# A state-space layer with four states side by side on the partitions, and a symmetric incidence matrix of which half is transposed instead of computed

## The chip, the core and the metric

The kernel runs on one core of a Trainium2 chip. The core has five engines with a queue of instructions each, and every queue is worked off in its order: PE (matrix products; its loads of the stationary operand are listed as PEld), DVE (vector work), ACT (activation functions and copies), POOL (a second, slower vector engine, which reads and writes SBUF only), and SP, which here only starts transfers (DMA). PE writes to PSUM, eight banks of 128 x 512 fp32; a tile of 128 x 512 fp32 fills one bank.

The metric is the time of one execution on the device in microseconds (us). Three runs of the kernel before took 5677.81, 5738.25 and 5755.19 us, with a median of 5738.25 us.

## The reference, cut to what matters

The program is a stack of four layers on a batch of 4 images with 128 channels and 64 x 64 pixels (4096 positions). Layers 2 and 3 (attention and mixtures of experts) are not touched by the change; only layers 0 and 1 are.

```python
# layer 0: a selective state-space scan, 256 inner channels d, 16 states n, along 4096 positions t
dA = exp(dt_t[:, :, None] * A)                         # A: 256 x 16
hn = dA * hprev + (dt_t * x_t)[:, :, None] * B_t[:, None, :]
y  = einsum('bdn,bn->bd', hn, C_t)                     # sum over the 16 states
...
y = (y + xc * D) * silu(zg);  out = y @ out_proj_w.T + x
# layer 1, on the group-normalised x: a hypergraph of 4096 tokens
d2 = sq[:, :, None] + sq[:, None, :] - 2.0 * einsum('bic,bjc->bij', xf, xf)
incidence = (sqrt(maximum(d2, 0)) < 16.0)              # 4096 x 4096 zeros and ones
edge = einsum('bve,bvc->bec', incidence, xe) / deg_e   # xe = xf @ W_fc.T + b_fc
vert = einsum('bve,bec->bvc', incidence, edge) / deg_v
out  = vert + xf;  then a batch norm over all images and silu
```

Two properties carry the change. In layer 0 each of the 256 x 16 scans is independent of the others, and B and C depend on the state and the position but not on the channel. In layer 1 the distances, and so the incidence matrix, are symmetric.

## The kernel before, in words

All matrix operands are fp32 but for the incidence matrix (zeros and ones in fp8) and the fp16 pairs (a high and a low part) that it is multiplied with.

**Layer 0** works on chunks of 512 positions: 8 chunks for each of 4 images. For a chunk, `before` issues four steps (load x; project through the convolution, L189 to L193; a small product that gives dt, B and C, L200 to L203; delta, L212 to L219). `state(s, n)` then handles one state for all 256 channels, which lie as two halves on the 128 partitions. A transfer on SP's queue (L235) spreads rows B and C of that state over all 128 partitions (tile `bt`, four buffers). POOL multiplies dt*x by B (`db`, L237, 128 x 1024). For each half ACT computes exp(dt*A) into a PSUM bank (`dA`, L241), and DVE runs the recurrence as a scan over 512 positions (`hs`, L243). ACT keeps the last column for the next chunk (`carry`, L245), DVE multiplies by C (`hc`, L247, 128 x 1024, all operands in SBUF), and PE sums over the states by two products with the identity matrix that accumulate in PSUM over the 16 states (`y`, L249). So a chunk has 16 states, 32 scans and 32 such products. `after` adds the skip term, multiplies by the gate on POOL (L258), projects out (L262), and stores the layer's output to device memory from ACT's queue.

**Layer 1** of an image builds the incidence matrix in 8 panels of 512 columns. A panel has 32 blocks of 128 x 512: `compare` computes a product on PE (`ps_g`, L358) and DVE compares it with the norms and writes zeros and ones (`inc`, L361). All 32 x 8 blocks are computed. `edges` multiplies the finished panel with the tokens (`ps_ed`, L370: 4 x 32 products of 258 columns a panel), in a PSUM bank of its own. Six of the eight panels are stored to device memory (L412) and loaded again (L423) for the second pass, which multiplies the panels with the edge features (`ps_v`, L436: 64 products of 512 columns a panel) in the same extra bank. The eight normalised chunks `xn` stay in SBUF from their load to the end of the image.

**The order of the work.** Layer 0 of image 0 is issued alone. Then layer 0 of image b+1 and layer 1 of image b are issued interleaved: after each of the 128 state steps as much of layer 1 is issued as its weighted work asks for. Layer 1 of image 3 stands alone at the end. The compiler's scheduler then fixes the order on each engine; tiles with the same tag share their buffers, and an instruction that needs a buffer waits for its last user. PSUM is divided into 3 banks `ps` for all passing products, 1 bank for `edges` and the second pass, 2 for `dA` and 2 for `y`.

Of the kernel before, what the change touches and what calls it, by code (L numbers as in the profile page):

```python
# [7 lines left out]
F32 = mybir.dt.float32  # L8
# [30 lines left out]
class Net:  # L39
# [33 lines left out]
    def layers01(self):  # L73
# [5 lines left out]
        with ExitStack() as ctx:  # L79
            wp = ctx.enter_context(tc.tile_pool(name="aw", bufs=1))  # L80
            w2 = ctx.enter_context(tc.tile_pool(name="l0p", bufs=2))
            bcp = ctx.enter_context(tc.tile_pool(name="l0bc", bufs=4))
            tp = ctx.enter_context(tc.tile_pool(name="l1t", bufs=2))
            dp = ctx.enter_context(tc.tile_pool(name="l0d", bufs=3, space=DRAM))
            ip = ctx.enter_context(tc.tile_pool(name="l1i", bufs=1, space=DRAM))

            ps = ctx.enter_context(tc.tile_pool(name="aps", bufs=3, space=PSUM))
            eps = ctx.enter_context(tc.tile_pool(name="l1e", bufs=1, space=PSUM))
            aps = ctx.enter_context(tc.tile_pool(name="l0a", bufs=2, space=PSUM))
            yps = ctx.enter_context(tc.tile_pool(name="l0y", bufs=1, space=PSUM))  # L90
# [8 lines left out]
            A = wp.tile([P, 2, DS], F32, tag="A", name="A")  # L99
            carry = wp.tile([P, DS, 2], F32, tag="carry", name="carry")  # L100
# [4 lines left out]
            top = wp.tile([P, 1], F32, tag="top", name="top")  # L105
            with tc.tile_pool(name="l0t", bufs=2) as tp0:
# [15 lines left out]
                nc.scalar.dma_start(A, a["L0_conv_A_log"].rearrange("(k p) n -> p k n", p=P))  # L122
                nc.scalar.activation(A, A, AF.Exp)
                nc.vector.tensor_scalar(A, A, -1.0, None, ALU.mult)
                for h in range(2):
# [13 lines left out]
                    self.transposed(ps, xpT[:, h, :], xw[:, h * P : (h + 1) * P])  # L139
# [28 lines left out]

            def before(b, c):
# [12 lines left out]
                def project():  # L182
                    xt = s["xt"]
                    xc = s["xc"] = w2.tile([P, 2, T], F32, tag="xc", name="xc")
                    zs = s["zs"] = w2.tile([P, 2, T], F32, tag="zs", name="zs")
                    for h in range(2):
# [4 lines left out]
                        pz = ps.tile([P, T], F32, tag="ps", name="ps_z")  # L191
                        nc.tensor.matmul(pz, wz[:, h, :], xt[:, 3:], start=True, stop=True)
                        nc.scalar.activation(zs[:, h, :], pz, AF.Silu)  # L193

                def small():
                    xc = s["xc"]
                    xd = s["xd"] = w2.tile([40, T], F32, tag="xd", name="xd")
# [5 lines left out]
                    nc.scalar.dma_start(bcd, xd[DR:40, :])  # L203

                def delta():

                    xd = s["xd"]
                    dl = s["dl"] = w2.tile([P, 2, T], F32, tag="dl", name="dl")
# [8 lines left out]
                    nc.gpsimd.tensor_tensor(dl, dl, sp, ALU.add)  # L217
                    dx = s["dx"] = w2.tile([P, 2, T], F32, tag="dx", name="dx")
                    nc.gpsimd.tensor_tensor(dx, dl, s["xc"], ALU.mult)  # L219

                return s, [load, project, small, delta]

            def state(s, n):


                c, dl, dx, bcd = s["c"], s["dl"], s["dx"], s["bcd"]
                if n == 0:
                    s["y"] = [yps.tile([P, T], F32, tag=f"y{h}", name=f"y{h}") for h in range(2)]
                y = s["y"]

                bt = bcp.tile([P, 2, T], F32, tag="bt", name="bt")
                rows = bass.AP(
                    tensor=bcd.tensor, offset=bcd[n : n + 1, :].offset, ap=[[0, P], [DS * T, 2], [1, T]]
                )
                nc.sync.dma_start(bt, rows)  # L235
                db = w2.tile([P, 2, T], F32, tag="db", name="db")
                nc.gpsimd.tensor_tensor(db, dx, bc(bt[:, 0, :], 2), ALU.mult)  # L237
                hs = w2.tile([P, 2, T], F32, tag="hs", name="hs")
                for h in range(2):
                    dA = aps.tile([P, T], F32, tag="dA", name="dA")  # L240
# [705 lines left out]
```

## Time and profile before

The profiled execution of the kernel before has a span of 5744.0 us from its first to its last instruction; the mean clock granted to PE in it is 0.881 of full speed.

| | us |
|---|---|
| median of three runs (5677.81 to 5755.19) | 5738.25 |
| span of the profiled execution | 5744.0 |
| PE busy (81% of the span) | 4672.7 |
| DVE busy (65%) | 3714.2 |
| POOL busy (32%) | 1836.1 |
| ACT busy (31%) | 1763.0 |
| moved by DMA, MB | 502.31 |

A row of the profile's list of groups reads: line, engine, operation, what it writes and reads, the shapes, how often; then its busy time in us, the mean length of one in ns, and the idle time of the engine just before it with the instruction that ended most of it. An fp32 product appears as two records, since PE takes two passes for it: 2048 records of L249 are 1024 products. Records of products overlap at their ends, so the distance from start to start, and not the length of a record, is what a product costs on a busy PE. The clock granted to PE varies; at full clock a pass of 512 columns starts every 0.43 us.

### The profile page before, as it was taken

Reading aid. Unit: us, or ns where it says so; the run is one execution under the profiler, and the core shown is the slowest. Engines: PE = TensorE matmul, PEld = TensorE weight load, DVE = VectorE, ACT = ScalarE, POOL = GpSimd, SP = SyncE. Lnnn points to the kernel's source line nnn. Section 1 sums busy time; section 2 is a strip of 40 time slices with the busy share of each in tenths; the row PEclk is TensorE's granted clock in tenths of the full one; section 3 lists DMA queues with packets and bytes.
Section 4 is the critical chain, followed back from the end, with each engine's and each line's share of the span. In section 5 each row is a group of like instructions: output and inputs, shape, how many; then the busy total and the mean of one; then the engine's idle time right before and its main releaser. Section 6 shows DMA issues by size and latency. Waiting matters only on the chain. (4 is left out here: it accounts for less than half of the span.)

```text
span 5744.0 us, 50270 instructions
## 1 busy us (share of the span) xinstructions
PE 4672.7 (81%) x18487; PEld 2474.2 (43%) x18487; DVE 3714.2 (65%) x5227; ACT 1763.0 (31%) x2956; POOL 1836.1 (32%) x916
## 2 busy tenths in 40 slices
PE   6676688888888888888888888899986667689779
PEld 2222244444434444443444444355544555358535
DVE  6889878877647777765777876556415455438610
ACT  4544543333224333232433333210013333312220
POOL 5555544443544444344434444410121000000000
PEclk8777899999999999998999999899997788769975
DMA  4344423332343334334333332511041000150052
GB/s 103 104 109 110 109 80 99 100 100 73 111 139 86 84 105 106 69 104 138 88 91 102 90 87 85 160 66 44 23 173 49 1 1 1 56 183 1 2 185 80
DMA packets 215081, 502.31 MB, mean 87 GB/s; under 512 B 16522, under 2 KB 19122, under 8 KB 208690
## 3 DMA queue, kind: packets, MB, share of 16 engines
q1 hardware_dynamic: 203538, 479.74, 29.2%
q10 hardware_dynamic: 11296, 19.37, 1.0%
q8 instruction: 145, 2.38, 0.2%
q14 instruction: 102, 0.84, 0.1%
HBM read 421.45 MB, written 77.59 MB: 87 GB/s over the span
## 5 line engine op out<-in xcount | busy, mean ns | idle before, releaser
L237 POOL TENSOR_TENSOR db<-dx,bt 128x1024 f32<-128x1024 f32 x512 | 1282.9, 2509 | 1342.5 <-DVE hs L243 674.8
L249 PE MATMUL y<-hc,cst 128*128 128x512 f32 x2048 | 1091.8, 659 | 195.2 <-DVE hc L247 189.1
L243 DVE TENSOR_TENSOR_SCAN hs<-dA,carry,db 128x512 f32<-128x512 f32 x896 | 1103.7, 1266 | 219.7 <-POOL db L237 177.4
L358 PE MATMUL ps_g<-xn 128*128 128x512 f32 x2048 | 973.1, 611 | 131.7 <-DVE inc L361 127.9
L241 ACT ACTIVATE dA<-dl,A 128x512 f32<-128x512 f32 x1024 | 701.7, 688 | 1186.6 <-DVE hs L243 1142.1
L247 DVE TENSOR_TENSOR hc<-hs,bt 128x1024 f32<-128x1024 f32 x512 | 877.5, 1714 | 276.4 <-PE y L249 272.9
L361 DVE SCALAR_TENSOR_TENSOR inc<-ps_g,hcl,hb 128x512 fp8e4<-128x512 f32 x1024 | 733.0, 742 | 144.5 <-PE ps_g L358 105.9
L249 PEld LDWEIGHTS y<-hc,cst 128*128 128x128 f32 x2048 | 405.0, 208 | 716.8 <-issue 372.6
L358 PEld LDWEIGHTS ps_g<-xn 128*128 128x128 f32 x2048 | 382.8, 194 | 655.9 <-issue 368.1
L370 PE MATMUL ps_ed<-xs,inc 128*128 128x258 f16 x4096 | 494.8, 277 | 67.0 <-DVE ed L375 66.9
L370 PEld LDWEIGHTS <-inc 128*128 128x128 fp8e4 x4096 | 403.7, 99 | 221.5 <-issue 162.9
L436 PE MATMUL ps_v<-inc_v,es 128*128 128x512 fp8e4 x1536 | 368.3, 395 | 0.0
L436 PEld LDWEIGHTS <-es 128*128 128x128 f16 x2048 | 206.9, 101 | 282.0 <-issue 82.1
L245 ACT COPY carry<-hs 128x2 f32<-128x2 f32 x448 | 86.3, 193 | 708.1 <-DVE hs L243 705.7
L262 PE MATMUL ps_o<-xc,opT 128*128 128x512 f32 x128 | 110.2, 1011 | 180.6 <-POOL xc L258 180.5
L189 PE MATMUL ps_c<-xt,wc 128*128 128x512 f32 x512 | 240.2, 608 | 1.1 <-DMA xt<-in_x 1.1
L217 POOL TENSOR_TENSOR dl<-dl,sp 128x1024 f32<-128x1024 f32 x32 | 81.0, 2532 | 417.5 <-ACT sp L216 417.5
L243 DVE TENSOR_TENSOR_SCAN hs<-dA,db 128x512 f32<-128x512 f32 x128 | 150.8, 1206 | 61.3 <-POOL db L237 55.6
L572 PE MATMUL ps_qkT<-cst,qkv 128*128 128x128 f32 x256 | 61.8, 421 | 150.5 <-DVE qkv L566 150.5
L382 POOL TENSOR_TENSOR ed<-ed,rdeg 128x512 f32<-128x512 f32 x32 | 48.9, 1529 | 393.2 <-DVE rdeg L380 393.2
L375 DVE TENSOR_TENSOR ed<-ps_ed,ed 128x129 f32<-128x129 f32 x128 | 36.4, 285 | 201.3 <-ACT ed L374 201.1
L189 PEld LDWEIGHTS ps_c<-xt,wc 128*128 128x128 f32 x512 | 100.4, 197 | 131.2 <-issue 123.8
(246 smaller groups left out, 5165.6 us busy)
## 6 DMA issues: line engine op xcount, KB each, us to landing
bt<-bcd SPq DMA_DIRECT2D x512, 512.0 KB
inc<-inc SPq DMA_DIRECT2D x24, 2048.0 KB
inc_v<-inc SPq DMA_DIRECT2D x24, 2048.0 KB
w<-in_L_ffn_weight SPq DMA_DIRECT2D x32, 1024.0 KB
w2f<-in_L_ffn_weight SPq DMA_DIRECT2D x32, 1024.0 KB
x<-x ACTq DMA_DIRECT2D x32, 256.0 KB
xn<-x SPq DMA_DIRECT2D x32, 256.0 KB
hg<-rb SPq DMA_DIRECT2D x32, 256.0 KB
```

The lines of the kernel that those rows point to most:

```text
L189: nc.tensor.matmul(pc, wc[:, h, j, :], xt[:, j : j + T], start=j == 0, stop=j == 3)
L237: nc.gpsimd.tensor_tensor(db, dx, bc(bt[:, 0, :], 2), ALU.mult)
L241: nc.scalar.activation(dA, dl[:, h, :], AF.Exp, scale=A[:, h, n : n + 1])
L243: nc.vector.tensor_tensor_scan(hs[:, h, :], dA, db[:, h, :], init, ALU.mult, ALU.add)
L245: nc.scalar.copy(carry[:, n, :], hs[:, :, T - 1])
L247: nc.vector.tensor_tensor(hc, hs, bc(bt[:, 1, :], 2), ALU.mult)
L249: nc.tensor.matmul(y[h], self.ident, hc[:, h, :], start=n == 0, stop=n == DS - 1)
L262: nc.tensor.matmul(po, opT[:, h, :], xc[:, h, :], start=h == 0, stop=h == 1)
L358: nc.tensor.matmul(pq, xn[v // 4][:, v % 4 * P : (v % 4 + 1) * P], xn[c], start=True, stop=True)
L361: nc.vector.scalar_tensor_tensor(inc[:, v, :], pq, hc[:, v : v + 1], hb, ALU.subtract, ALU.is_gt, saturate=False)
L370: nc.tensor.matmul(pe[:, : 2 * P + 2], inc[:, v, i * P : (i + 1) * P], xs[:, v, :], start=v == 0, stop=v == NB - 1,)
L436: nc.tensor.matmul(pv, es[:, e, k, :], inc[:, e, :], start=e == 0 and k == 0, stop=e == NB - 1 and k == 1,)
```

## The change

In layer 0, a step no longer covers one state of 256 channels. It covers four states of 64 channels: the partitions hold four states of 32 channels each, and two such groups of 32 channels lie side by side in a tile (`step(s, h, q, k)`: half h, four states q, pair k of groups). There are still 16 steps a chunk, with two scans of 512 positions and one product 128 x 1024 with B and with C each. For this layout dt and dt*x, which are needed on four partition groups, are stored to device memory (`dd`, 16 small transfers a chunk) and loaded spread (`r`, 1 MB, 4 a chunk); B and C are loaded for four states at a time (`bt`, 8 a chunk instead of 16). The exponentials and the scans work in place in PSUM (`hs`, 2 tiles of 2 banks). In every third step (5 of 16 in a chunk) the scan writes to SBUF instead (`ho`) and the product with C runs on POOL; in the others DVE computes it from PSUM. The sum over states becomes one product with `fold`, a 128 x 32 stationary matrix that adds the four states; four of these, for four groups of 32 channels, write to the four quarters of the partitions of one PSUM bank, after every second step. The addition in delta moves from POOL to DVE, the gate is computed in its own step on the current chunk, the tail `after` is issued one chunk later, and all stores of the layer move from ACT's queue to SP's.

In layer 1, a block of panel c that lies above the diagonal is taken from the panel that holds its mirror image: four fp8 products with a 128 x 128 fp8 identity (`turn`) transpose the four 128 x 128 pieces of it into a PSUM bank, and ACT copies that bank to fp8. So 144 of the 256 blocks of an image are computed and 112 are turned. The panels needed for it are loaded in pieces of 256 KB from device memory (21 an image), except the one just before, which is still in SBUF. The second pass loads and normalises its chunk of x again. The extra PSUM bank is gone: `edges` and the second pass take their banks from the three `ps`, and `edges` is issued in quarters between the steps of the next panel. Layer 1's preparation (`norm`, `tokens`) is issued step by step during the first chunk of the next image's layer 0, and the main part from the 12th step on.

The diff, cut to its core:

```diff
+            hps = ctx.enter_context(tc.tile_pool(name="l0h", bufs=2, space=PSUM))
+            yps = ctx.enter_context(tc.tile_pool(name="l0y", bufs=1, space=PSUM))
             ps = ctx.enter_context(tc.tile_pool(name="aps", bufs=3, space=PSUM))
-            eps = ctx.enter_context(tc.tile_pool(name="l1e", bufs=1, space=PSUM))
-            aps = ctx.enter_context(tc.tile_pool(name="l0a", bufs=2, space=PSUM))
-            yps = ctx.enter_context(tc.tile_pool(name="l0y", bufs=1, space=PSUM))
...
+            nc.vector.tensor_copy(id8, self.ident, saturate=False)
+            nc.vector.tensor_tensor(fold, self.ident[:, 0:32], self.ident[:, 32:64], ALU.add)
+            for i in (2, 3):
+                nc.vector.tensor_tensor(fold, fold, self.ident[:, 32 * i : 32 * i + 32], ALU.add)
...
-                    nc.scalar.dma_start(bcd, xd[DR:40, :])
+                    nc.sync.dma_start(bcd, xd[DR:40, :])
...
-                    nc.gpsimd.tensor_tensor(dl, dl, sp, ALU.add)
-                    dx = s["dx"] = w2.tile([P, 2, T], F32, tag="dx", name="dx")
+                    nc.vector.tensor_tensor(dl, dl, sp, ALU.add)
+                    dx = sp
                     nc.gpsimd.tensor_tensor(dx, dl, s["xc"], ALU.mult)
 
+                    dd = s["dd"] = [
+                        dp.tile([32, 2, 2, T], F32, tag=f"dd{k}", name=f"dd{k}") for k in range(4)
+                    ]
+                    for k in range(4):
+                        for i, t in enumerate((dl, dx)):
+                            for j in range(2):
+                                p0 = 64 * (k % 2) + 32 * j
+                                nc.sync.dma_start(dd[k][:, i, j, :], t[p0 : p0 + 32, k // 2, :])
...
+            def spread(s, k):
+
+                r = w2.tile([P, 2, 2, T], F32, tag="r", name="r", bufs=3)
+                dd = s["dd"][k]
                 rows = bass.AP(
-                    tensor=bcd.tensor, offset=bcd[n : n + 1, :].offset, ap=[[0, P], [DS * T, 2], [1, T]]
+                    tensor=dd.tensor, offset=dd[0:1, 0, 0, :].offset, ap=[[0, 4], [4 * T, 32], [1, 4 * T]]
                 )
-                nc.sync.dma_start(bt, rows)
+                nc.sync.dma_start(r.rearrange("p i j t -> p (i j t)"), rows)
+                return r
+
+            def rates(s, q):
+
+                bt = w2.tile([P, 2, T], F32, tag="bt", name="bt", bufs=3)
+                bcd = s["bcd"]
+                rows = bass.AP(
+                    tensor=bcd.tensor, offset=bcd[8 * q : 8 * q + 1, :].offset, ap=[[2 * T, 4], [0, 32], [1, 2 * T]]
+                )
+                nc.sync.dma_start(bt.rearrange("p i t -> p (i t)"), rows)
+                return bt
+
+            def step(s, h, q, k):
+
+
+                c = s["c"]
+                i = (8 * h + 2 * q + k) % 3
+                if q == 0:
+                    s["r"][2 * h + k] = spread(s, 2 * h + k)
+                if k == 0:
+                    s["bt"] = rates(s, q)
+                    s["hc"] = []
+                r, bt = s["r"][2 * h + k], s["bt"]
                 db = w2.tile([P, 2, T], F32, tag="db", name="db")
-                nc.gpsimd.tensor_tensor(db, dx, bc(bt[:, 0, :], 2), ALU.mult)
-                hs = w2.tile([P, 2, T], F32, tag="hs", name="hs")
-                for h in range(2):
-                    dA = aps.tile([P, T], F32, tag="dA", name="dA")
-                    nc.scalar.activation(dA, dl[:, h, :], AF.Exp, scale=A[:, h, n : n + 1])
-                    init = 0.0 if c == 0 else carry[:, n, h : h + 1]
-                    nc.vector.tensor_tensor_scan(hs[:, h, :], dA, db[:, h, :], init, ALU.mult, ALU.add)
+                nc.gpsimd.tensor_tensor(db, r[:, 1, :, :], bc(bt[:, 0, :], 2), ALU.mult)
+                hs = hps.tile([P, 2, T], F32, tag="hs", name="hs")
+                pool = i == 1
+                ho = w2.tile([P, 2, T], F32, tag="ho", name="ho", bufs=1) if pool else hs
+                for j in range(2):
+                    kk = 4 * h + 2 * k + j
+                    nc.scalar.activation(hs[:, j, :], r[:, 0, j, :], AF.Exp, scale=Ar[:, kk, q : q + 1])
+                    init = 0.0 if c == 0 else carry[:, q, kk : kk + 1]
+                    nc.vector.tensor_tensor_scan(ho[:, j, :], hs[:, j, :], db[:, j, :], init, ALU.mult, ALU.add)
...
-                hc = w2.tile([P, 2, T], F32, tag="hc", name="hc")
-                nc.vector.tensor_tensor(hc, hs, bc(bt[:, 1, :], 2), ALU.mult)
-                for h in range(2):
-                    nc.tensor.matmul(y[h], self.ident, hc[:, h, :], start=n == 0, stop=n == DS - 1)
+                hc = w2.tile([P, 2, T], F32, tag="hc", name="hc", bufs=4)
+                (nc.gpsimd if pool else nc.vector).tensor_tensor(hc, ho, bc(bt[:, 1, :], 2), ALU.mult)
+                s["hc"].append(hc)
+                if k == 1:
+                    if q == 0:
+                        s["y"] = yps.tile([P, T], F32, tag="y", name="y")
+                    for j in range(4):
+                        nc.tensor.matmul(
+                            s["y"][32 * j : 32 * j + 32, :], fold, s["hc"][j // 2][:, j % 2, :],
+                            start=q == 0, stop=q == 3, skip_group_check=True,
+                        )
...
-                nc.scalar.dma_start(self.x1[b][:, c * T : (c + 1) * T], x1)
+                nc.sync.dma_start(self.x1[b][:, c * T : (c + 1) * T], x1)
...
+                def turn(inc, src, v):
+
+
+                    w = v % 4
+                    pt = ps.tile([P, CH], F32, tag="ps", name="ps_tu")
+                    for i in range(4):
+                        nc.tensor.matmul(
+                            pt[:, i * P : (i + 1) * P], src[:, i, w * P : (w + 1) * P], id8, start=True, stop=True
+                        )
+                    nc.scalar.copy(inc[:, v, :], pt, saturate=False)
+
                 def edges(inc, ed, c, i):
 
 
-                    pe = eps.tile([P, CH], F32, tag="e", name="ps_ed")
+                    pe = ps.tile([P, CH], F32, tag="ps", name="ps_ed")
                     for v in range(NB):
...
+                        if v % 8 == 7 and v < NB - 1:
+                            yield 8 * 260
...
+                def panel(inc, hb, c, last):
+                    piece = {}
+                    for v in (x for pair in zip(range(16), range(16, 32)) for x in pair):
+                        if v < 4 * c:
+                            g = v // 4
+                            if g not in piece:
+                                if g == c - 1:
+                                    piece[g] = last[:, 4 * c : 4 * c + 4, :]
+                                else:
+                                    piece[g] = tp.tile([P, 4, CH], FP8, tag="piece", name="piece", bufs=2)
+                                    nc.sync.dma_start(piece[g], panels[g][:, 4 * c : 4 * c + 4, :])
+                            turn(inc, piece[g], v)
+                            yield 8 * P
+                        else:
+                            compare(inc, hb, c, v)
+                            yield 4 * CH
...
-                    pv = eps.tile([P, CH], F32, tag="e", name="ps_v")
+                    pv = ps.tile([P, CH], F32, tag="ps", name="ps_v")
...
+            lag = 12
...
```

## The prediction

> **What bounds the kernel now.** I first cut the trace where layers change hands: layer 0 of image 0 alone (from 50 to 733 us), three stretches of layer 0 beside layer 1, layer 1 of image 3 alone (3773 to 4275), and the rest up to layer 3, which the change does not touch. Busy time by stretch (us; PE, PEld, DVE, ACT, POOL, then PE's granted clock):
>
> ```profile
> core 0: us, PE busy (x) PEld busy (x) DVE busy (x) ACT busy (x) POOL busy (x), PEclk, DMA share, GB/s
> 50.00:733.00 683.00, 460.01 (x760) 160.68 (x760) 607.18 (x429) 332.00 (x529) 415.96 (x158) 0.80 0.44 110
> 733.00:1757.00 1024.00, 871.30 (x3028) 422.35 (x3028) 736.31 (x770) 330.92 (x577) 450.96 (x217) 0.93 0.36 99
> 1757.00:2781.00 1024.00, 871.96 (x3029) 423.37 (x3028) 731.21 (x769) 330.51 (x575) 445.61 (x216) 0.93 0.36 99
> 2781.00:3773.00 992.00, 851.96 (x2987) 415.23 (x2986) 714.45 (x756) 311.49 (x547) 423.81 (x207) 0.93 0.36 99
> 3773.00:4275.00 502.00, 481.36 (x2260) 273.91 (x2260) 231.56 (x353) 39.43 (x82) 56.32 (x65) 0.98 0.17 63
> 4275.00:5744.00 1469.00, 1099.09 (x6336) 761.72 (x6336) 682.96 (x2106) 400.11 (x624) 40.31 (x48) 0.77 0.18 62
> ```
>
> The head is DVE's (89% busy), the three middle stretches PE's (85%) with DVE at 71%, the tail PE's (96%). Next the groups of the stretch 1757 to 2781, which give prices and counts for one image:
>
> ```profile
> L249 PE MATMUL y<-hc,cst 128*128 128x512 f32 x513 | 254.2, 616 | 7.0 <-DVE hc L247 5.0 <-DVE xc L255 1.9
> L358 PE MATMUL ps_g<-xn 128*128 128x512 f32 x512 | 249.4, 618 | 43.8 <-DVE inc L361 42.6 <-ACT xc L190 0.8 <-DVE x L263 0.3
> L247 DVE TENSOR_TENSOR hc<-hs,bt 128x1024 f32<-128x1024 f32 x128 | 200.2, 1564 | 95.3 <-PE y L249 94.7
> L361 DVE SCALAR_TENSOR_TENSOR inc<-ps_g,hcl,hb 128x512 fp8e4<-128x512 f32 x256 | 180.6, 740 | 38.6 <-PE ps_g L358 33.9
> ```
>
> The sums over states and the distance products are 504 of PE's 872 us, and the change cuts both. Last the timeline of the head, where one state takes 4.75 us:
>
> ```profile
> 506.93 2.34 POOL L237 TENSOR_TENSOR db<-dx,bt 128x1024 f32<-128x1024 f32 x1 [4.62 <-DVE hs L243]
> 507.89 2.46 DVE L247 TENSOR_TENSOR hc<-hs,bt 128x1024 f32<-128x1024 f32 x1
> 510.27 2.44 DVE L243 TENSOR_TENSOR_SCAN hs<-dA,carry,db 128x512 f32<-128x512 f32 x2
> 512.64 2.46 DVE L247 TENSOR_TENSOR hc<-hs,bt 128x1024 f32<-128x1024 f32 x1
> ```
>
> `hc` takes 1.19 us at its shortest (median 1.23), but 2.46 here: it ends about 1.1 us after POOL's `db`, as if it began to work only then. Both read two SBUF operands. DVE work with one operand in PSUM is not stretched (L361: 715 to 753 ns in all 1024).
>
> **Layer 0, part by part.** *Sums over states.* Before, 2 products a step, 256 an image. After, also 256, but of 32 columns, four to the four quarters of a bank. Layer 2 has such products:
>
> ```profile
> 4998.37 1.92 PE L822 MATMUL ps_h<-w,pooled 128*32 128x512 f32 x16 [0.39 <-DVE pooled L806]
> ```
>
> 16 records are 8 products, in 1.92 us at full clock: two groups of four, each 0.86 us, the time of one full product. So 64 groups x 0.86 = 55 us an image in place of 254. Switching between forms: elsewhere in layer 2, at half clock, the last full-width pass before a 32-column one holds PE 0.99 us, where passes come every 0.85, so 0.13 us a switch; 128 switches are 17 us. I take 72. The Trainium skill (TensorEngine Tiling (Array Packing), "Key Properties") says that a change of tiling mode drains the engine, and gives no price; that speaks against interleaving these products. With nothing for it the sum below would be 17 us an image less; no run here shows the alternation itself.
>
> *Product with C.* 88 of 128 an image stay on DVE, from PSUM. Nearest rows: L255 (SBUF with PSUM, 512 elements, 0.73 us) and L375 (PSUM with SBUF, 129 elements, 0.285); on their line 1024 elements take 1.33 us, and L247 itself takes 1.19 unstretched. Bounds: 1.19, and 1.56 if the stretching stays. I take 1.26, between the first two, as L361 and L255 are never stretched: 111 us for 200. 40 go to POOL at 2.35 (L237's median), 94 us. *The scan in PSUM* is not in the trace (it reads PSUM, writes SBUF, 1.21 to 1.27 us). Bounds: 1.15, its shortest, and 1.6; I take 1.25, since ACT writes PSUM and SBUF at one price (L241 and L190, 0.69 us each).
>
> *Chain of a chunk.* DVE: 32 scans x 1.25 + 11 x 1.26 + skip term, tail and delta's addition 4.1 = 58 us. POOL: 21 x 2.35 + 2.35 + 2.4 = 54. Neither can run alone: in the built order POOL's product with C stands behind the next step's `db` and waits for its scan, and the `db` after it waits too, while DVE waits for that `db`. One piece of that, from the end of step 5's `db` at 0 (step 4 is POOL's): DVE runs scan 5a, 4b, 5b (to 3.75) and product 5 (to 5.0); POOL waits for scan 4b until 2.5, runs product 4 to 4.85 and step 6's `db` to 7.2; only then can DVE scan 6a, after 2.2 us of waiting. Walking all 16 steps through both lists in this way I got 72 us (14 of it DVE's waits); before, 683/8 = 85. The new path dt -> device memory -> `r` (dx 2.35, 16 issues x 0.36, a landing, 1 MB at `bt`'s 512 KB in 3.5 us: 18 us) has six steps of cover (27 us); only the first chunk shows it, +10. Head: 50 + 10 + 8 x 72 + 5 (the last tail) = 641 us instead of 733.
>
> **Layer 1.** 112 of 256 distance products go: PE 249 x 112/256 = 109 us, DVE 180.6 x 112/256 = 79 less per image. Each turned block adds four fp8 products of 128 columns. Nearest: `edges` (L370), 32 of 258 columns in 3.74 us, 0.117 each, with fp8 weight loads of 98 ns. Bounds: 0.058 (by columns) and 0.117; I take 0.10, the weight load, so 448 x 0.10 = 45 us. ACT's copy of a bank takes 0.59 (L431): 66 us an image on an engine with 330 of 1024 busy, but in line with the exponentials. Pieces, second loads and 2.35 us here and there of POOL lie beside other work, as DMA is 36% busy; uncovered, 21 pieces at some 3 us are 63 us an image.
>
> **Sum for a middle stretch.** PE: 872 - 254 + 72 - 109 + 45 = 626. DVE: 731 - 89 - 79 + 14 (addition of delta) = 577. POOL: 446 + 94 - 36 (delta's addition gone, `db` no longer stretched) = 504. ACT: 331 + 66 + 16 (some 7 more table loads of 1.28 us, 8 more normalised chunks of 0.8) = 413. If the busiest engine is 85% busy as before: 626/0.85 = 736. The other way: chunk chain 72, plus layer 1's DVE work (577 - 8 x 58)/7.25 = 16 and POOL's (504 - 8 x 54)/7.25 = 10 standing in between, 98 us for the 7.25 chunks in which layer 1 runs, and 54 for the rest: 764. I take 764, since the chain is what four queues in order cannot shorten. Tail: (481 - 99 + 45)/0.96 = 445, plus 20 because `edges` now takes one of the three banks: 465. The rest stays at 1469.
>
> 641 + 3 x 764 + 465 + 1469 = 4867, say **4870 us**, against 5744 of the profiled execution; the median of the runs (5738.25) is the same within 0.1%. About 2% is what a measurement tells from no change.
>
> **Rivals.** (1) *Looser coupling*: the waits in the chain are filled by layer 1's work, PE at 97%: 645 a stretch, tail 450, **4500 us**. For it: DVE had 29% to spare. Against: four queues in order, each with the others' results in front. Chance 0.12. (2) *ACT in lockstep*: turned blocks wait on ACT for PE, with exponentials and `carry` (for which `hc` now waits, as both read the same bank) behind them. A turn stands behind 8 `edges` products (0.94 us) or a distance product (0.86) or both, some 1.3 us; 112 x 1.3 = 146 a stretch, **5300 us**. For it: ACT's row for `ed` waiting on `ps_ed` (62 waits, 375.6 us), and only two banks turn over while `edges` holds the third. 0.26. (3) *The four products do not overlap*: 64 x 3 x 0.86 = 165 more on PE a stretch, 791/0.85 = 930, **5370 us**. L822 is against it, and its own place differs only in the switching. 0.04. (4) *No difference (within 2%)*, (2) and (3) together or scans at 1.6: 0.05. (5) *Slower*: SP's queue starves layer 0. Every transfer, the 16 stores of a chunk and the pieces, now stands in one line with `r` and `bt`, and one that waits holds all. Its longest wait before was 49.3 us (for `inc`, L412). Held so once a chunk, the path is 18 + 49 - 27 = 40 us late, x 32 = 1280: **6150 us**; it decides from 31 us a chunk on (the sum then passes 5860). Against: SP waited 327 us for `inc` before too, in the same line as `bt`, and POOL's waits for `bt` were 147 us a stretch. 0.08.
>
> The forecast's own case (4680 to 5060) has 0.45. The range 4550 to 5400 leaves out (5), (4) and half of (1). Faster by over 2%: 0.12 + 0.45 + 0.26 + 0.04 = 0.87; within 2%: 0.05; slower: 0.08.
>
> **What would show it.** `y` in groups of four with starts 0.01 us apart; `hc` on DVE near 1.26 us with a narrow spread; scans near 1.25; layer 1 of image 0 starting near 640; stretches near 764 with DVE and PE at 75 to 85%. Rival 2 shows as exponentials idle behind copies that wait for `ps_tu`; rival 5 as POOL waiting for `r` and `bt`. I am wrong if DVE's scans in PSUM cost 1.5 us or more (1024 scans: +256 us), or if the granted clock falls below 0.8 because PE idles more: 626 is at 0.93.

## The result and the profile after

The changed kernel is slower. Its median is 5997.99 us (four runs, 5970.85 to 6020.19) against 5746.72 us of the kernel before beside it (four runs, 5677.81 to 5764.49). The ratio is **1.0486, with a 95% interval of 1.0404 to 1.0569**. The forecast was 4870 us, with a range of 4550 to 5400. The profiled execution after has a span of 6018.1 us.

First the stretches, cut at the same events as before: layer 0 of image 0 alone, three stretches of layer 0 beside layer 1, layer 1 of image 3 alone, the rest. The columns are busy time of PE, PEld, DVE, ACT and POOL, then PE's granted clock, the mean busy share of the 16 DMA engines, and GB/s.

```profile
50.00:966.00 916.00, 336.49 (x760) 67.47 (x758) 462.64 (x395) 311.34 (x512) 442.79 (x198) 0.59 0.27 95
966.00:2012.00 1046.00, 755.99 (x3250) 336.59 (x3248) 578.36 (x622) 412.41 (x709) 481.69 (x256) 0.85 0.33 112
2012.00:3075.00 1063.00, 755.99 (x3252) 334.13 (x3252) 580.73 (x625) 414.32 (x711) 485.82 (x256) 0.85 0.33 111
3075.00:4113.00 1038.00, 755.73 (x3226) 335.85 (x3226) 572.59 (x617) 397.78 (x690) 476.41 (x252) 0.84 0.32 108
4113.00:4561.00 448.00, 428.82 (x2483) 265.30 (x2482) 143.42 (x238) 106.92 (x201) 54.88 (x64) 0.96 0.23 86
```

In a middle stretch three engines have about the work that was forecast (in brackets): DVE 573 to 581 us (577), ACT 398 to 414 (413), POOL 476 to 486 (504). PE has 756 in place of 626. Yet the stretches take 1038 to 1063 us, not 764, with PE busy for 71 to 73% of them. In the first stretch no engine is busy for more than 51% of the time. What is lost is lost wherever layer 0 runs; the tail, where it does not, takes 448 us (465 was forecast).

Next the groups of the page that answer to those shown of before (`y`, distance products, product with C, comparison), over all four images:

```profile
L308 PE MATMUL y<-hc,fold 128*32 128x512 f32 x2048 | 613.6, 743 | 537.1 <-DVE hc L302 365.6
L438 PE MATMUL ps_g<-xn 128*128 128x512 f32 x1152 | 630.2, 652 | 122.9 <-DVE inc L441 84.5
L441 DVE SCALAR_TENSOR_TENSOR inc<-ps_g,hcl,hb 128x512 fp8e4<-128x512 f32 x576 | 421.8, 741 | 193.6 <-PE ps_g L438 185.7
L302 DVE TENSOR_TENSOR hc<-hs,bt 128x1024 f32<-128x1024 f32 x352 | 425.0, 1213 | 183.9 <-ACT carry L300 164.7
```

The product with C takes 1.21 us from PSUM (before, 1.71 on average over all four images and 1.56 in the stretch shown), and 144 of 256 comparisons are left. The work shrank; the waits grew. The chain of causes is in the list of waits (engine, line, what ended the wait: us in total, times, longest):

```profile
DVE hs L297 <- POOL db L289: 701.3, 167, 32.9
POOL db L289 <- DMA r<-dd: 674.9, 76, 28.0
ACT hs L295 <- DMA r<-dd: 646.1, 85, 17.8
...
POOL db L289 <- DMA bt<-bcd: 350.9, 79, 11.9
```

POOL waits 1026 us for the two loads of layer 0, ACT 646 for one of them, and DVE's scans wait 701 for POOL. Now what the transfers do in 100 us of the first stretch (500 to 600 us), in 40 equal slices: the busy share of the 16 engines in tenths, and the rate.

```profile
DMA  2222222226322225222012232222222002355222
GB/s 103 103 110 105 105 103 105 105 105 235 118 108 108 101 99 175 102 100 88 10 34 92 86 83 66 69 66 85 90 103 87 5 0 52 78 134 146 63 102 103
```

This is the line that matters. The share stands at "2" in most slices, and where nothing else moves the rate stands at 103 to 105 GB/s. It looks like a quarter of the capacity, idle for the rest; it is **four engines of sixteen, full**. In the records of the packets from 400 to 960 us, a packet of `r` (8192 bytes) or `bt` (4096 bytes) is in flight 84% of the time, and then 3.9 of them at a time on average; for 69% of the time it is exactly four. Four packets of 8192 bytes in 311 ns each are 105 KB/us (105 GB/s), just the rate of the slices. The records do not name the engine of a packet; that four packets at a time are four engines is inferred, and the probe at the end of the experiments bears it out. In the source pattern of both loads the outermost dimension is 4, the states.

### The profile page after: what moved, and what is told of

The parts are those of the page before. It is cut to its first block, busy times and chain, and to the rows that moved or that the text cites. A ratio compares the mean times of both kernels' runs of the same rounds, so it can differ in the third digit from the quotient of the medians.

```text
span 6018.1 us, 52668 instructions
## 1 busy us (share of the span) xinstructions
PE 4147.3 (69%) x19383; PEld 2108.1 (35%) x19383; DVE 3034.5 (50%) x4661; ACT 2058.3 (34%) x3467; POOL 1982.1 (33%) x1076
## 5 line engine op out<-in xcount | busy, mean ns | idle before, releaser
L289 POOL TENSOR_TENSOR db<-r,bt 128x1024 f32<-128x1024 f32 x512 | 1199.7, 2350 | 1425.1 <-DMA r<-dd 674.9
L295 ACT ACTIVATE hs<-r,Ar 128x512 f32<-128x512 f32 x1024 | 704.1, 691 | 1629.3 <-DMA r<-dd 646.1
L297 DVE TENSOR_TENSOR_SCAN hs<-hs,carry,db 128x512 f32<-128x512 f32 x616 | 783.5, 1282 | 913.6 <-POOL db L289 600.6
L308 PE MATMUL y<-hc,fold 128*32 128x512 f32 x2048 | 613.6, 743 | 537.1 <-DVE hc L302 365.6
L438 PE MATMUL ps_g<-xn 128*128 128x512 f32 x1152 | 630.2, 652 | 122.9 <-DVE inc L441 84.5
L441 DVE SCALAR_TENSOR_TENSOR inc<-ps_g,hcl,hb 128x512 fp8e4<-128x512 f32 x576 | 421.8, 741 | 193.6 <-PE ps_g L438 185.7
L302 DVE TENSOR_TENSOR hc<-hs,bt 128x1024 f32<-128x1024 f32 x352 | 425.0, 1213 | 183.9 <-ACT carry L300 164.7
L302 POOL TENSOR_TENSOR hc<-ho,bt 128x1024 f32<-128x1024 f32 x160 | 375.9, 2349 | 358.8 <-DVE ho L297 290.5
L297 DVE TENSOR_TENSOR_SCAN ho<-hs,carry,db 128x512 f32<-128x512 f32 x280 | 355.7, 1270 | 148.0 <-POOL db L289 125.1
L454 ACT CAST inc<-ps_tu 128x512 fp8e4<-128x512 f32 x448 | 253.7, 585 | 179.9 <-PE ps_tu L451 178.8
```

What stands on the lines that cost most here:

```text
L289: nc.gpsimd.tensor_tensor(db, r[:, 1, :, :], bc(bt[:, 0, :], 2), ALU.mult)
L295: nc.scalar.activation(hs[:, j, :], r[:, 0, j, :], AF.Exp, scale=Ar[:, kk, q : q + 1])
L297: nc.vector.tensor_tensor_scan(ho[:, j, :], hs[:, j, :], db[:, j, :], init, ALU.mult, ALU.add)
L302: (nc.gpsimd if pool else nc.vector).tensor_tensor(hc, ho, bc(bt[:, 1, :], 2), ALU.mult)
L308: nc.tensor.matmul(s["y"][32 * j : 32 * j + 32, :], fold, s["hc"][j // 2][:, j % 2, :], start=q == 0, stop=q == 3, skip_group_check=True,)
L438: nc.tensor.matmul(pq, xn[v // 4][:, v % 4 * P : (v % 4 + 1) * P], xn[c], start=True, stop=True)
```

## The experiments

Three theories were to be told apart. **A**: a load whose outermost dimension is 4 is carried by four DMA engines, and its transfer time sets layer 0. **B**: SP's single line, with stores that wait for results, holds the loads back (the mechanism of the forecast's fifth rival). **C**: the chain of four engines in order is slow by itself and the transfers are hidden.

### Another order of the partitions

```diff
-  r:  ap=[[0, 4], [4 * T, 32], [1, 4 * T]]
+  r:  ap=[[4 * T, 32], [0, 4], [1, 4 * T]]
-  bt: ap=[[2 * T, 4], [0, 32], [1, 2 * T]]
+  bt: ap=[[0, 32], [2 * T, 4], [1, 2 * T]]
   fold and Ar built for partition = 4 * channel + state
```

> The changed kernel with another order of the partitions in layer 0: partition 4*channel+state in place of 32*state+channel. The loads `r` and `bt` keep their number, place and bytes; only the outermost dimension of their source is now 32 channels and no longer 4 states (`fold` and the rates are laid out to fit). Theory A (a load whose outermost dimension is 4 is carried by 4 of the 16 DMA engines: some 104 KB/us in the trace of the changed kernel, so that the 8 MB of a chunk take about 80 us of transfer): `r` lands in 2.5 to 4 us and no longer 10, the stretch of layer 0 alone falls from 955 us to 600 to 720, the three middle stretches from 1010-1035 to 760-880, and the whole to 4800-5300 us. Theory B (SP's one line: 16 stores, `bcd`, the store of `x1` and the pieces hold `r` and `bt` back by their waits): nothing of that is touched, so 5850-6100 us. Theory C (the chain of four engines in order, ACT's turned blocks and POOL's products, is what is slow, and the transfers are hidden): 5850-6100 us as well.

**5091.48 us**, ratio to before 0.8885 (0.8816 to 0.8953). Past the preparation of the weights, the instructions of every engine and their order are those of the changed kernel (PE's, POOL's and SP's are the same from the first to the last; on DVE a clearing of `xt` of 0.06 us is recorded ahead of a scan in one and beside it in the other, twice), and so are the bytes of the two loads. Only the access pattern differs, and it is worth 964 us between the two spans (6018.1 and 5054.6). B and C both forecast 5850 to 6100 us. The stretches, and the same 100 us of transfers:

```profile
50.00:701.00 651.00, 339.85 (x760) 68.04 (x759) 459.43 (x395) 311.17 (x512) 443.40 (x198) 0.62 0.39 134
701.00:1537.00 836.00, 713.00 (x3248) 323.59 (x3248) 577.14 (x622) 412.26 (x708) 480.54 (x255) 0.92 0.41 140
...
3197.00:3646.00 449.00, 430.51 (x2482) 265.76 (x2482) 143.01 (x237) 106.91 (x201) 54.59 (x64) 0.95 0.24 85
```

```profile
DMA  1255398001866814740340140840700024532980
GB/s 26 57 144 139 124 428 341 0 0 26 347 259 224 333 69 153 217 157 0 51 159 0 36 174 0 279 167 0 210 3 0 0 52 106 142 98 82 437 347 0
```

The second fence is the one to set beside that of the changed kernel: bursts at up to 437 GB/s with empty slices between them, in place of a steady 105. `r` and `bt` are in flight 37% of the head's time (300 to 690 us), 12.8 packets at once; in the middle stretches it is 30%, where the changed kernel had 76%. A chunk in the head takes 78.8 us where it took 111 (here and below: from the first scan of a chunk to that of the next, median of the second to the seventh chunk of image 0).

### The same loads, cut into four

```diff
-  nc.sync.dma_start(r, rows)             # 4 x 32 rows
+  for a4 in range(4):
+      nc.sync.dma_start(r[32 * a4 : 32 * a4 + 32], rows_32)     # bt likewise
```

> The changed kernel with each load `r` and `bt` cut into four, one for each 32 partitions; the same bytes and the same order of partitions, but 48 loads a chunk on SP's queue in place of 12 (36 more issues at some 0.36 us, 13 us a chunk). Theory A: the outermost dimension is 32, all engines carry each load, and the time falls to 4850-5400 us. Theory B: more in the line that is the bound, 6100-6500 us. Theory C: unchanged, 5850-6100 us.

5863.10 us, ratio 1.0233 (1.0179 to 1.0286): a miss for A (4850 to 5400) and for B, and just inside C's range (5850 to 6100). A chunk in the head does fall, from 111 to 92.5 us, and 12.2 packets of `r` are now in flight at once. But each takes 593 ns (median up to 4200 us) where it took 312 in the changed kernel and 309 in the interleaved one. The last probe below bears on that. The two loads no longer fill the time: from 300 to 780 us a packet of them is in flight 45% of it. The middle stretches stay near 1065 us. The scheduler set another order on every engine for this kernel, so that the remainder can't be put down to one thing; it stays open. Taken alone this run would speak for C; it is the first experiment, with the order unchanged, that rules C out as the cause of the loss.

### The converse on the kernel before

```diff
-  bt: ap=[[0, 128], [16 * T, 2], [1, T]]
+  bt: ap=[[0, 4], [0, 32], [1, 2 * T]]      # rows of B and C made neighbours
```

> The converse, on the kernel before: its `bt` (128 partitions, all the same two rows) is read through a pattern of outermost dimension 4 (4 x 32 x one piece of 4096 bytes; the rows of B and C of a state are made neighbours, as in the changed kernel, so that a partition has one piece of 4096 bytes and not two of 2048). Nothing else is changed. Theory A: 512 KB at 103 KB/us are 5.1 us, 16 of them 82 us a chunk, beside a chunk of 85 us in the head; with the rest of a chunk's transfers some 90 to 100 us a chunk, 6000-6500 us in all. Theories B and C: the number of issues and their order are as before, 5650-5850 us.

5871.54 us, ratio 1.0239 (1.0175 to 1.0303): more than B and C forecast (up to 5850), less than A did (from 6000). The order on POOL, ACT and SP is that of the kernel before. The direction is A's, the size of the whole is not. In the head the trace shows A's mechanism: from 300 to 760 us a packet of `bt` is in flight 99% of the time, 3.9 at once, and a chunk takes 88.4 us where it took 85.3. By the packets (16 loads of 128, 167 ns each on average) four engines need 86 us a chunk. So the transfers had just passed the chain that they stand beside, which fits how little is lost. POOL's waits for `bt` go from 457.7 to 1292.2 us (before, then this run):

```profile
POOL db L237 <- DMA bt<-bcd: 457.7, 120, 14.5
POOL db L244 <- DMA bt<-bcd: 1292.2, 315, 15.9
```

The changed kernel has the same 8 MB of such loads a chunk, beside a chain that was walked at 72 us, and less room to issue ahead: three buffers for the four `r` of a chunk, and a way through device memory ahead of the first. There `r` and `bt` are in flight for 84% of the 111 us, some 94 us a chunk. How its other 17 us divide was not measured apart.

### SP's line relieved

```diff
-  nc.sync.dma_start(dd..., bcd, x1)
+  nc.scalar.dma_start(dd..., bcd, x1)
```

> The changed kernel with the 16 stores of dt and dt*x, the store `bcd` and the store of `x1` issued by ACT's queue and no longer SP's: 18 of the 36 issues of a chunk leave SP's line, and with them the waits for DVE's and POOL's results ahead of `r` and `bt`. Theory A: the transfers are as slow as before, 5700-6100 us. Theory B: `r` and `bt` are issued in time, 4900-5400 us. Theory C: ACT, in line with the exponentials, waits for these results too, 6000-6400 us.

6261.22 us (four runs: 6242.34 to 6271.78 and one of 6340.76), ratio 1.0916 (1.0846 to 1.0987), slower than the changed kernel. B's gain (4900 to 5400) did not come; the time also lies above A's range (5700 to 6100) and in C's (6000 to 6400). In the head `r` and `bt` are in flight 78% of the time (400 to 1060 us). The scheduler's order changed here too, so this run alone would not settle it; with the first experiment, in which SP's line is the same instruction by instruction and 964 us go, B is not the cause.

### Layer 1's part, in the interleaved version

```diff
-  if v < 4 * c:        # take the block from its mirror image
+  if False:            # compute all 256 blocks
```

> The interleaved version (5091 us) with the turned blocks undone: all 256 distance products and comparisons of an image are computed again, none of the 112 blocks is turned, no pieces are loaded; everything else of the change stays. The forecast's account (four queues in order; layer 1's DVE work stands between layer 0's): 79 us of DVE more and 64 us of PE more an image (109 back, 45 saved), 66 us of ACT less: a stretch 835 -> 890-930, the stretch of image 3's layer 1 alone 449 -> 485, in all 5250-5450 us. Rival (the turned blocks cost in ACT's line what they save elsewhere): within 2% of 5091 us or less, 4900-5190.

5301.80 us, ratio 0.9272 (0.9203 to 0.9342): 210 us more than with the turned blocks. The rival fails, and the account of the forecast holds, though the tail grew by more than was expected (505 us, not 485). First line a middle stretch (836 us with turned blocks), second the tail (449):

```profile
703.00:1588.00 885.00, 769.72 (x3032) 335.62 (x3030) 651.14 (x734) 358.67 (x599) 485.85 (x257) 0.93 0.36 127
...
3360.00:3865.00 505.00, 493.43 (x2260) 278.28 (x2260) 227.65 (x351) 44.64 (x89) 54.79 (x64) 0.97 0.17 65
```

DVE has 74 us more, PE 57 more, ACT 54 less; a stretch is 49 us longer and the tail 56.

### POOL's product with C

```diff
-  pool = i == 1
+  pool = False
```

> The interleaved version with every product with C on DVE, none on POOL (5.3 of 16 a chunk move). The forecast's account (POOL's product stands ahead of the next `db` and waits for its scan, DVE then waits for that `db`: 14 us of DVE's waits a chunk): POOL 54 -> 42 us a chunk, DVE 58 -> 65; the chunk in the head falls from 79 to 70-75 us, in all 4800-5040 us. Rival (DVE's busy time sets the chunk): 6.4 us more a chunk, 5150-5350 us.

**4880.94 us**, ratio 0.8551 (0.8493 to 0.8609), 210 us below the interleaved version; a chunk in the head takes 69.5 us in place of 78.8. DVE gets 37 us more work in the first stretch, and the stretch still ends 73 us earlier:

```profile
50.00:628.00 578.00, 344.23 (x757) 67.66 (x756) 496.21 (x436) 311.51 (x511) 350.46 (x158) 0.64 0.43 150
628.00:1431.00 803.00, 711.78 (x3256) 319.60 (x3254) 616.95 (x664) 420.14 (x714) 393.02 (x216) 0.94 0.42 147
```

That speaks for the forecast's account, but the scheduler also set another order on every engine with this edit, and what of the 210 us belongs to the order was not measured apart.

The same edit on the changed kernel, with its four-engine loads:

> The changed kernel as it was (partition 32*state+channel, the loads on four DMA engines) with every product with C on DVE: the same edit that took 210 us from the interleaved version. Theory A (while `r` and `bt` come at some 104 KB/us their transfers set the chunk, and what the engines save is hidden): within 2% of 5998 us, 5880-6120. If the engines' order set the chunk here too: 210 us less, 5700-5850.

5965.92 us, ratio 1.0422 (1.0330 to 1.0515), within 1% of 5997.99: the chunk in the head takes 112 us beside 111. Its first stretch:

```profile
50.00:960.00 910.00, 336.94 (x752) 68.45 (x750) 491.60 (x428) 309.54 (x507) 343.82 (x155) 0.60 0.27 94
```

PE, POOL and SP have the same instructions in the same order as in the run above, which took 4880.94 us; the pattern of the two loads parts them by 1085 us. What the engines save is hidden as long as the transfers set the pace. That is A once more, from the other side.

### Three attempts to go on from there

> The interleaved version with four buffers for `bt` in place of three (and three for `hc` in place of four, for the room): its loads can be issued one group of two steps earlier. If landings still end POOL's waits (idle time before `db` that no engine ends: some 10 us a chunk in the head): a chunk 79 -> 70-74 us, 4750-4950 us. If the loads are now in time and the engines' order sets the chunk: 5000-5150 us.

5112.86 us, ratio 0.8959 (0.8897 to 0.9022): no gain (the edit: four buffers for `bt`, three for `hc`). Landings no longer set the chunk, unless the missing buffer for `hc` took back what they gave; the next run has four of each, in the version without POOL's product.

> The interleaved version with all products with C on DVE and, in the room of `ho`, a fourth buffer for `bt`. If landings still hold POOL (226 us of `db`'s idle time that no engine ends, in the version with three buffers): 4700-4830 us. If DVE sets the chunk (88% busy in the head): within 1% of 4881 us.

4868.22 us, ratio 0.8539 (0.8458 to 0.8621): not to be told from 4880.94. These two are the fastest of all runs; both beat both kernels.

> The interleaved version with all products with C on DVE and the addition of delta back on POOL (2.5 us a chunk on DVE, 2.35 on POOL). If DVE's busy time sets the chunk of the head (494 of 560 us): 2.5 us a chunk less in the head and up to as much in the stretches, 4800-4870 us. If the path through POOL sets it: 4880-4960 us.

4934.99 us, ratio 0.8639 (0.8578 to 0.8700): 54 us more than 4880.94, 1%, with intervals that overlap, so no difference is shown. The gain did not come. DVE was 86% busy in the first stretch, and taking 2.5 us a chunk from it didn't help: a chunk takes 71.1 us there. The time lies where the second theory had it (the path from delta through POOL); that this path sets the chunk is not shown.

### The pattern alone

> The interleaved version without POOL's product, with a probe put ahead of its weights: one tile of 128 x 8192 bytes is stored and loaded back one load at a time, three times each, the next one only when DVE has read one element of the last. The patterns of the source: 128 rows; 32 rows, each four times (the interleaved `r`); and rows repeated as a block 16, 8, 4 (the changed kernel's `r`) and 2 times, so that the outermost dimension is 16, 8, 4, 2; then 32 rows alone and 64 rows alone, each into as many partitions. Theory A (as many engines as the outermost dimension has, up to 16, each with packets of 311 ns): 128 packets take 2.5 us of transfer for 128, 32 and 16; 5.0 for 8; 10.0 for 4; 19.9 for 2, with the same fixed time before and behind. Rival (the repeated source rows are slow, whatever the outermost dimension): 32x4 and the four blocks alike, some 10 us, only 128 rows fast. The 32 rows alone: 0.6 us at 311 ns a packet, or 1.2 if the 593 ns of the split loads come from their going into 32 partitions only. The whole: some 200 us above 4881.

Each line is DVE's read of one element when a load has landed; in brackets how long DVE waited. The order is: 128 rows; 32 rows, each four times; blocks repeated 16, 8, 4 and 2 times; 32 rows alone; 64 rows alone.

```profile
12.65 0.15 DVE L100 COPY got<-big 128x1 f32<-128x1 f32 x1 [8.40 <-DMA big<-src]
17.86 0.15 DVE L102 COPY got<-big 128x1 f32<-128x1 f32 x1 [5.06 <-DMA big<-src]
25.46 0.15 DVE L104 COPY got<-big 128x1 f32<-128x1 f32 x1 [7.45 <-DMA big<-src]
37.69 0.15 DVE L106 COPY got<-big 128x1 f32<-128x1 f32 x1 [12.08 <-DMA big<-src]
57.41 0.15 DVE L108 COPY got<-big 128x1 f32<-128x1 f32 x1 [19.57 <-DMA big<-src]
80.20 0.15 DVE L110 COPY got<-big 128x1 f32<-128x1 f32 x1 [22.64 <-DMA big<-src]
83.61 0.14 DVE L112 COPY got<-big 32x1 f32<-32x1 f32 x1 [3.25 <-DMA big<-src]
88.38 0.15 DVE L114 COPY got<-big 64x1 f32<-64x1 f32 x1 [4.64 <-DMA big<-src]
93.45 0.15 DVE L100 COPY got<-big 128x1 f32<-128x1 f32 x1 [4.92 <-DMA big<-src]
```

(The first line's wait holds the store as well; the last is the same load in the next round.) The whole took 5125.11 us, one run. From the packets of the first round:

| outermost dimension | in flight | ns a packet (median) | first to last packet, us |
|---|---|---|---|
| 128 rows | 13.7 | 309 | 3.4 |
| 32, each four times | 14.0 | 309 | 3.3 |
| 16 blocks | 14.9 | 618 | 4.8 |
| 8 blocks | 8.0 | 637 | 9.6 |
| 4 blocks | 3.6 | 530 | 17.4 |
| 2 blocks | 2.0 | 313 | 20.8 |
| 32 rows, 32 partitions | 10.0 | 396 | 1.4 |
| 64 rows, 64 partitions | 13.8 | 598 | 2.5 |

The number in flight follows the outermost dimension: 2, 4, 8, and up to 16 from there. The rival (repeated rows are slow) falls with the second line: each row is read four times there too, and the load is as fast as 128 different rows. The length of a packet is a second effect that A didn't have: A expected 2.5 us for 16 blocks and 10.0 for 4, and it took 4.8 and 17.4.

> The second probe, in the same place: with four engines the load took longer (some 17 us of transfer) than 128 packets of 311 ns over four engines would (10.0), and packets of the blocks of 16, 8 and 4 took some 530 to 640 ns. Two causes to tell apart. (1) The engines read the same rows at the same time: then outermost dimension 16 and 4 with 128 different rows (row stride ordered so) take 2.5-3.5 us and 10-11 us, and the repeated blocks of 16 and 4 some 4.8 and 17. (2) It is the dimension 16 or 4 itself, or where the packets go: then different rows are no faster than repeated ones. Beside it 64 rows into partitions 0 to 63 (2.5 us of transfer before, 570 ns a packet) and into every other partition of 128, and 32 rows into every fourth: if the number of neighbouring partitions makes the packets slow, the spread ones take 309 ns a packet and half the time. In all some 150 us above 4881.

The lines, in order: 16 outermost with repeated rows; 4 outermost with 128 different rows, then with repeated ones; 64 rows into partitions 0 to 63, and into every other partition; and, from the second round, 16 outermost with different rows (in the first round its wait holds the store too).

```profile
22.05 0.15 DVE L102 COPY got<-big 128x1 f32<-128x1 f32 x1 [6.88 <-DMA big<-src]
40.61 0.15 DVE L104 COPY got<-big 128x1 f32<-128x1 f32 x1 [18.41 <-DMA big<-src]
59.29 0.15 DVE L106 COPY got<-big 128x1 f32<-128x1 f32 x1 [18.53 <-DMA big<-src]
64.14 0.15 DVE L108 COPY got<-big 64x1 f32<-64x1 f32 x1 [4.70 <-DMA big<-src]
67.89 0.15 DVE L110 COPY got<-big 128x1 f32<-128x1 f32 x1 [3.60 <-DMA big<-src]
...
78.31 0.15 DVE L100 COPY got<-big 128x1 f32<-128x1 f32 x1 [7.17 <-DMA big<-src]
```

Different rows (7.17 and 18.41 us) are no faster than repeated ones (6.88 and 18.53), so the source isn't what makes the packets long. Where they go is: 64 rows into every other partition take 309 ns a packet and 1.9 us from first to last, into neighbouring ones 528 ns and 2.5 us. The split loads went into 32 neighbouring partitions each, and their 593 ns fit that; but one such load alone had 396 ns (the table's row), so that the whole of the 593 is not shown. For 32 rows into every fourth partition the median stayed at 439 to 458 ns, so that half of the expectation did not come.

## Why the prediction was wrong

**The step that failed** is the one on the new path in "Chain of a chunk": "a landing, 1 MB at `bt`'s 512 KB in 3.5 us", with six steps of cover (27 us) for 18 us. The price was carried over from a load with another access pattern: before, the outermost dimension of `bt` was 128. The new `r` needs 10.0 us of transfer by its packets (128 x 312 ns over four engines), not 7, and `bt`, whose new pattern was not looked at, 5.1 instead of 3.5 (128 x 159 ns over four). For one `r` alone that would be 21 us, still inside the 27 us of cover. But the loads share the four engines, and the sum over a chunk was never made. Four `r` and eight `bt` at the assumed rate are 4 x 7 + 8 x 3.5 = 56 us, safely below the chain's 72; at the measured medians they are 4 x 10.0 + 8 x 5.1 = 81 us, above it (89 us by the mean lengths in the head, 357 and 168 ns), and they become the bound before any latency or wait for a buffer is added. The other half of the same error is the sentence that second loads lie beside other work "as DMA is 36% busy". A share over 16 engines says nothing of a load that can use four. Of the 0.27 in the head after, `r` and `bt` make up 0.20: four engines of sixteen, for 84% of the time.

The Trainium skill (DMA: Bandwidth & Descriptors, "Why a DMA increments its semaphore by 16 and not by 1") says that the number of engines is the largest number up to 16 that divides the slowest dimension of both patterns. The packets in flight agree: 3.9 in the head of the changed kernel, and 2.0, 3.6, 8.0 and 14.9 in the probe for 2, 4, 8 and 16. An estimate by that page would have been four engines for `r` and `bt`; the prediction didn't apply it.

**The fifth rival** had the right sign (6150 us forecast, 5998 measured) and nearly the right size (40 us a chunk; 964 us between the spans with and without the pattern are 30 us for each of 32 chunks), but the wrong mechanism, so the nearness is luck. It put the delay on waits in SP's line. That line is the same, order and all, in the version that is 964 us faster. Its sign, POOL waiting for `r` and `bt`, came too: it cannot tell a load that is issued late from one that is slow.

**What held once the pattern was mended.** Against the interleaved version, whose profiled execution has 5054.6 us:

| | forecast | changed kernel | interleaved |
|---|---|---|---|
| head, to the end of layer 0 of image 0 | 641 | 966 | 701 |
| a middle stretch | 764 | 1038 to 1063 | 825 to 836 |
| tail | 465 | 448 | 449 |
| rest | 1469 | 1457 | 1409 |

- *Durations.* `hc` from PSUM 1.21 us (1.26 taken), the scans in PSUM 1.28 (1.25), POOL's products 2.35, ACT's copy 0.585 (0.59). The stretching of POOL's products is gone: `db` takes 2.33 to 2.38 us in all 512.
- *Turned blocks.* Their products are 34.1 + 11.5 = 46 us a stretch on PE, as forecast (45). The second rival, ACT in lockstep, is refuted by the tail and by the run without turning.
- *`y`* was mis-sized: 72 us a stretch forecast, 133.9 measured (the stretch from 1537 to 2372 us). The four products of a group wait for two `hc`, and the scheduler's order puts work of other kinds between them:

```profile
1802.82 0.38 PE L458 MATMUL ps_tu<-id,piece 128*128 128x128 fp8e4 x4 [1.50 <-DVE inc L448]
1803.13 1.05 PE L315 MATMUL y<-hc,fold 128*32 128x512 f32 x2
1804.11 1.12 PE L445 MATMUL ps_g<-xn 128*128 128x512 f32 x2
...
1805.95 1.05 PE L315 MATMUL y<-hc,fold 128*32 128x512 f32 x4
```

  The first `y` line is one product (two records), the last is two side by side, in the same 1.05 us. In the stretch the 64 groups of four fall apart into 28 pieces of one product, 43 of two, 10 of three and 25 of four, all with a median of 1.05 to 1.07 us, and two longer ones. The products do overlap, as forecast; they don't come together. From its start to the next start of another kind a piece costs 0.98 us, near the 0.86 + 0.13 that the forecast took for a group with one switch: the price held, the number of pieces (108 in place of 64) did not. With distance products at 156 us (140) and `edges` at 146 (125), that is 99 us more, against the 90 by which PE's 716 exceed the 626 (`ps_o`'s records got 11 us shorter).
- *The chain of a chunk*: 72 us walked, 78.8 measured in the interleaved head. The cross chain through POOL's product, described there as 14 us of DVE's waits a chunk, fits what was measured: without it (and with another order) the chunk takes 69.5 us, and 210 us go in all.
- *The clock* was named as a way to be wrong, and it did fall to 0.59 in the head. It is a companion, not the cause: it is 0.62 in the interleaved head, which is 265 us shorter.

## What to carry to other kernels

Put a large dimension outermost in the source of every large load (32 and 128 took 3.3 and 3.4 us in the probe, 16 took 4.8 and 4 took 17.4), here by choosing which of two indices runs fastest on the partitions, and let the load reach all 128 partitions; and price a new load by a row whose access pattern is the same, not by one with the same bytes. Read a DMA share against the engines that the loads can use: here a steady share near 0.25 with an unchanging rate was a full pipe of four. Add up the transfers of one round of a loop and set the sum beside the chain of that round before calling them hidden.

## What the runs showed of the hardware that was not expected

- Two loads of the same bytes to the same 128 partitions took 5 and 19 us, by the order of two dimensions alone. From the first to the last packet (17.4 and 3.3 us) the factor is 5.3, larger than the 4 of the number of engines, since the packets are longer as well: 530 ns in place of 309 with four blocks.
- Into 64 neighbouring partitions a packet of 8192 bytes takes 517 to 617 ns (medians of the six rounds of both probes), into every other one of 128 it takes 309. The Trainium skill (SBUF — State Buffer, "Door 1: The DMA port swizzle") says that the rate depends on how many of 16 ports the partitions reach, and its table gives partitions 0 to 63 eight of them; the two rows agree. If each engine takes a run of neighbouring partitions, the same table would put the engines of the 16, 8 and 4 blocks two to a port and those of the 2 blocks one to a port, and the 618, 637, 530 and 313 ns fit. That is argued; no run tried it with other partitions.
- In the changed kernel itself the packets of `r`, with the same pattern, had a median of 312 ns, not the 530 of the probe. Why is open.
- The rest of the program, which no version touches, took 1469 us before, 1457 after and 1409 in the interleaved version, with PE's granted clock at 0.77, 0.78 and 0.82. What gives the later layers a better clock stays open.
